# Layer 0's values from the copied projection, and one transposition for the source terms of four blocks

## The chip, the cores and the metric

The kernel runs on one core of a Trainium2 chip. The metric is device time in microseconds (us), from one launch to its end; several runs are taken and the median counts.

## What is computed

Two layers of attention on a graph, over a batch of 16 images with 1024 nodes of 256 features each. `adj` is a 1024 x 1024 matrix of zeros and ones per image.

```python
# layer 0: x = layernorm(x + gnn0(x, adj))
h = einsum('bnd,hde->bhne', x, W)                    # 4 heads of 64
e_src = einsum('bhne,hte->bhtn', h, a_src)           # source terms
e_dst = einsum('bhne,hte->bhtn', h, a_dst)
weight = where(adj == 1, leaky_relu(e_src[..., :, None] + e_dst[..., None, :], 0.01), -1e9)
dst = softmax(weight) @ h + bias
out = relu(dst) + h                                  # then a layer norm per head
# layer 1: x = layernorm(x + gnn1(x, adj))
qkv = layer_norm(x).split_heads(8)                   # queries, keys and values are the same
attn = softmax(where(adj > 0, qkv @ qkv.T / sqrt(32), -inf)) @ qkv
x = x + attn
x = x + gelu(layer_norm(x) @ W1 + b1) @ W2 + b2
```

The kernel uses that exp(leaky_relu(s + d)) is a maximum of two products: after a factor common to a row is taken out, a weight of layer 0 is max(cb, dinv) * mask, where cb comes from the source terms (`exp(0.99 * e_src)`, a row over the queries, the same on all partitions) and dinv from the destination terms (`exp(-0.99 * e_dst)`, one number per partition). The values of layer 0 are `(h + bias) * exp(e_dst)` for each head, with `exp(e_dst)` itself as a 65th column that gives the sums.

## The kernel before

**Streams.** The program is written out in Python for all 16 images. Two generators, `layer0` and `layer1`, are interleaved by a loop at the end of `fast_path` (lines 1014 to 1032): while layer 1 of image b runs (`attention1`, then `mlp`), layer 0 of image b + 1 runs beside it (`prepare`, then `attention0`). The loop asks a model of the engines, the class `Pace` (lines 90 to 173), which of the two can go on, and follows a course (`COURSE`, line 999) that says how far layer 0 should be for each place of layer 1. Shorter pieces, called chains, are begun with `begin` and run when `Pace` believes that what they need is there (`advance`), or at once when somebody needs their result or their buffer (`complete`, `settle`). The order on each engine is then fixed: the engines work off their queues in that order and wait on semaphores. All engines' instructions are recorded on line 61, so the profile names tiles and not lines.

**Layer 0, prepare** (lines 484 to 540) goes over the eight blocks of 128 nodes of an image in pairs (`GB` = 2):
- four transposes of x to `xT` on TensorE, copied by ScalarE;
- `turn_mask` for each block: eight transposes of the adjacency block `ak`, and a ScalarE instruction that writes the mask; it also issues the load of a later adjacency block on GpSimd's queue;
- for each block, two matmuls of `xT` with `w0e` give a bank `ph` of 264 columns: h (256), the destination terms (4), the source terms (4). ScalarE takes from it, in this order, the source terms, `exp` of the destination terms twice, and h into `hb`;
- `values0` on VectorE: an add (tile `z`) and a multiplication into `v0`;
- `turn_sources` after each pair: makes rows out of the source terms, takes their exponential and stores them to `esr` in DRAM on SyncE's queue. After four blocks the first two factors `cb` are loaded back from `esr`, spread over all partitions (`spread_factor`).

The banks of PSUM that prepare uses are two, `acc0` and `acc1` (`bank0`, lines 370 to 375); `attention0`'s accumulation, the transposes of layer 1's outputs (tiles `oT`, `o`) and of its normalised inputs (`sq`) use the same two. Tiles that carry chains are completed before their bank is taken again. The framework orders any two engines' accesses to one bank.

**Layer 0, attention0** (lines 567 to 626): VectorE makes 128 x 512 weights `p` from cb, dinv and mask, and TensorE multiplies them with `v0` into `acc`. `residual0` and `after0` do the head norms and the norm ahead of layer 1.

**Layer 1, attention1** (lines 722 to 804): 32 steps an image, each of four logits matmuls into `ps`, four exponentials on ScalarE, two mask products on VectorE and the products into `po`, three steps behind. Then `mlp`, with `hid`.

In the trace each image has a turn, where `mlp` of one image ends and `attention1` of the next begins, and prepare starts at about the same place.

Of the kernel before, what the change touches and what calls it, by code (L numbers as in the profile page):

```python
# [31 lines left out]
F32 = mybir.dt.float32  # L32
# [3 lines left out]
AF = mybir.ActivationFunctionType  # L36
# [3 lines left out]
P = 128  # L40
# [136 lines left out]
def fast_path(  # L177
# [24 lines left out]
    nc = Pace(tc.nc)  # L202
    B, N, D = x.shape
    H0, _, HO = w0.shape
# [9 lines left out]
    BPH = HALF // P  # L214
    Q = 32
# [3 lines left out]
    GB = 2  # L219
# [6 lines left out]
    const = ctx.enter_context(tc.tile_pool(name="const", bufs=1))  # L226
    def ring(name, bufs, **kwargs):
        return Ring(nc, ctx.enter_context(tc.tile_pool(name=name, bufs=bufs, **kwargs)), bufs)

    one, two, three, four, eight = [  # L230
        ring(n, i) for n, i in (("one", 1), ("two", 2), ("three", 3), ("four", 4), ("eight", 8))
    ]
# [11 lines left out]
    ident = const.tile([P, P], F32, name="ident")  # L244
# [22 lines left out]
    for c in range(DC):  # L267
        for h in range(H0):
            nc.scalar.dma_start(w0e[:, c, h * HO : (h + 1) * HO], w0[h, c * P : (c + 1) * P, :])

    apart = [const.tile([P, H0, Q], F32, name=f"apart{g}") for g in range(GB)]
    for t in apart:
        nc.vector.memset(t, 0.0)
    terms = ((a_src, nc.sync, w0e[:, :, D + H0 : D + 2 * H0]), (a_dst, nc.scalar, w0e[:, :, D : D + H0]))

    at = one.tile([P, 3, PAIR, HO, T], F32, name="v0")
    vectors = [at[:, i, :, :, :] for i in range(3)] + [one.tile([P, PAIR, HO, T], F32, name="xl")]
    for i, (src, queue, _) in enumerate(terms):
        for pair in range(H0 // PAIR):
# [3 lines left out]
                    tensor=src.tensor,  # L283
# [5 lines left out]
    def rows(queue, src, name):  # L289
        t = const.tile([P, D], F32, name=name)  # L290
        queue.dma_start(t, bass.AP(tensor=src.tensor, offset=src.offset, ap=[[0, P], [1, D]]))
        return t

    bias0_r = rows(nc.scalar, bias0, "bias0_r")
    for i, (_, _, dst) in enumerate(terms):
        for c in range(DC):
            t = two.tile([P, H0, HO], F32, name="z")
# [72 lines left out]
    def bank0(shape, dtype=F32):  # L370
        i = min((i for i in range(2) if not banks0[i]["busy"]), key=lambda i: banks0[i]["taken"])
        for chain in banks0[i]["readers"]:
            complete(chain)
        banks0[i].update(readers=[], taken=1 + max(bank["taken"] for bank in banks0))
        return ps_a.tile(shape, dtype, f"acc{i}"), banks0[i]
# [13 lines left out]
    def transpose_rows(dst, src, scale=None, shift=None):  # L389

        pt = side_bank([P, DC, GB, P])
        for g in range(GB):
            for c in range(DC):
                nc.tensor.transpose(pt[:, c, g, :], src[:, g, c * P : (c + 1) * P], ident)
        pt = pt.rearrange("p c g q -> p c (g q)")
        if scale is None:
            nc.scalar.copy(dst, pt)
        else:
            for c in range(DC):
                nc.scalar.activation(  # L400
                    dst[:, c, :], pt[:, c, :], AF.Identity, bias=shift[:, c : c + 1], scale=scale[:, c : c + 1]
                )
# [13 lines left out]
    def uses(chain, tile):  # L416
        users.setdefault(tile, []).append(chain)
# [13 lines left out]
    def begin(chain, engine, *needs):  # L431
        for n in needs:
            if not callable(n):
                uses(chain, n.tensor.name)
        chains.append([chain, engine, needs])

    def run(item):
        running.append(item[0])
        step = next(item[0], None)
        running.pop()  # L440
        if step is None:
            chains.remove(item)
        else:
            item[1:] = step[0], step[1:]
# [13 lines left out]
    def complete(chain):  # L458

        for item in list(chains):  # L460
            if item[0] is chain:
                while item in chains:
                    run(item)
# [8 lines left out]
    def load_adj(i):  # L472
        b, k = divmod(i, NB)
        if b < B:
            ak = adj_blocks[i] = three.tile([P, N], BF16, name="ak")
            nc.gpsimd.dma_start(ak, adj[b, k * P : (k + 1) * P, :])

    def load_blocks(i):
        b, k = divmod(i, NB // GB)
        if b < B:  # L480
            xk = x_blocks[i] = two.tile([P, GB, D], F32, name="xk")
            load_x(xk, b, k * GB, GB)

    def prepare(b, hb, esr, cbs, v0, dinv, mask):

        def turn_mask(k):
            i = b * NB + k  # L490
            ak = adj_blocks.pop(i)
            pt, _ = bank0([P, NB, P], BF16)
            for j in range(NB):
                nc.tensor.transpose(pt[:, j, :], ak[:, j * P : (j + 1) * P], identb)
            nc.scalar.activation(
                mask[k // BPH][:, :, k % BPH * P : (k % BPH + 1) * P],
                pt,
                AF.Square,
                bias=shift_c,
                scale=-(NEAR0 + NEAR1),  # L500
                accum_out=types[:, i : i + 1],
            )
            load_adj(i + 3)

        turning, scaling = [], []
        for k in range(0, NB, GB):
            i = b * (NB // GB) + k // GB
            load_blocks(i + 1)
            xk = x_blocks.pop(i)
            xT = one.tile([P, DC, GB * P], F32, name="xT")  # L510
            transpose_rows(xT, xk)
            yield 0.45, bank0_ready
            turn_mask(k)
            yield 0.5, bank0_ready, xT
            if k % BPH == 0:

                finish_norms(b - 1, k // BPH)
                hb.append(one.tile([P, BPH, D], F32, name=f"hb{k // BPH}"))
            for g in range(GB):
                if g == 0:  # L520

                    for chain in turning:
                        complete(chain)
                ph, _ = bank0([P, D + 2 * H0])
                for c in range(DC):
                    nc.tensor.matmul(ph, xT[:, c, g * P : (g + 1) * P], w0e[:, c, :], start=c == 0, stop=c == DC - 1)
                nc.scalar.copy(apart[g][:, :, 0], ph[:, D + H0 : D + 2 * H0])
                nc.scalar.activation(v0[:, k + g, :, HO], ph[:, D : D + H0], AF.Exp)
                nc.scalar.activation(dinv[:, k + g, :], ph[:, D : D + H0], AF.Exp, scale=-0.99)
                scaling.append(values0(v0[:, k + g, :, :], ph))  # L530
                begin(scaling[-1], "vector", ph)
                nc.scalar.copy(hb[-1][:, (k + g) % BPH, :], ph[:, 0:D])
                yield 0.9, bank0_ready
                if g == 0:
                    turn_mask(k + 1)
                    yield 0.5, bank0_ready, xT
            turning.append(turn_sources(esr, k, cbs))
            begin(turning[-1], "tensor", bank0_ready, *apart)
        for chain in turning + scaling:
            complete(chain)  # L540

    def turn_sources(esr, k, cbs):
        es, _ = bank0([P, GB, P])
        for g in range(GB):
            nc.tensor.transpose(es[:, g, :], apart[g].rearrange("p h q -> p (h q)"), ident)
        rows = two.tile([P, GB * P], F32, name="rows")
        nc.scalar.activation(rows, es.rearrange("p g q -> p (g q)"), AF.Exp, scale=0.99)
        nc.sync.dma_start(esr[:, k * P : (k + GB) * P], rows[0:P:Q, :])
        if k + GB == BPH:
            for at in ((0, 0), (0, 1)):  # L550
                cbs[at] = spread_factor(esr, *at)
        yield from ()

    def values0(v, ph):
        t = two.tile([P, H0, HO], F32, name="z")
        nc.vector.tensor_add(t.rearrange("p h e -> p (h e)"), ph[:, 0:D], bias0_r)
        nc.vector.tensor_mul(v[:, :, 0:HO], t, v[:, :, HO : HO + 1].to_broadcast([P, H0, HO]))
        yield from ()

    def spread_factor(esr, n, pair):  # L560

        cb = two.tile([P, PAIR, HALF], F32, name="cb")
        rows = esr[pair * PAIR : (pair + 1) * PAIR, n * HALF : (n + 1) * HALF]
        nc.sync.dma_start(cb, bass.AP(tensor=rows.tensor, offset=rows.offset, ap=[[0, P], [N, PAIR], [1, HALF]]))
        return cb
# [374 lines left out]
    def finish_norms(b, n):  # L940
        for chain in [c for at, c in norms.items() if at[:2] == (b, n)]:
            complete(chain)
# [537 lines left out]
```

## Time and profile before

| what | us |
|---|---|
| median of 3 runs | 3459.49 |
| lowest and highest of the runs | 3459.29, 3473.02 |
| the profiled execution | 3472.71 |
| its span, first to last instruction | 3470.9 |
| mean granted clock of TensorE | 0.979 of full speed |
| TensorE busy | 3321.2 |
| VectorE busy | 2982.8 |
| ScalarE busy | 1937.3 |

How to read the profile: PE is TensorE's matmul, PEld its loading of weights, DVE VectorE, ACT ScalarE, POOL GpSimd, SP SyncE. A group of instructions is written as output tile, arrow, input tiles, with shape and count, then busy time in us and the mean of one in ns, then the idle time of its engine just before, with what ended it. "The waits" are sums of that idle time by who waited and who ended it, with the number of times and the longest. "The chain" is followed back from the last instruction: at each step to what released it. A busy TensorE is not TensorE at its peak, since a matmul that waits in the pipeline counts as busy. Times within an execution count from the span's start.

### The profile page before, as it was taken

The numbers are of one execution on the slowest core, as the hardware profiler recorded it, in microseconds if no ns is written. First come the engines' busy times: TensorE is split into PE (matmuls) and PEld (weight loads), VectorE is DVE, ScalarE is ACT, GpSimd is POOL, SyncE is SP. The second block draws the span as 40 slices with busy tenths as digits, with TensorE's granted clock in tenths as the row PEclk, the third lists the DMA queues.
The fourth block names the chain that finished last, engine by engine and source line by source line (L and its number), as shares of the span: only waits on it lengthen the run. The fifth ranks groups of instructions, "written<-read, shape, count | busy, mean of one in ns | idle before, by whom it ended". The sixth has DMA issues, their size and how long they took to land.

```text
span 3470.9 us, 141029 instructions
## 1 busy us (share of the span) xinstructions
PE 3321.2 (96%) x64161; PEld 2259.7 (65%) x64161; DVE 2982.8 (86%) x5262; ACT 1937.3 (56%) x4192; POOL 418.9 (12%) x424
## 2 busy tenths in 40 slices
PE   5799999999999999999999999999999999999998
PEld 5458576675856758576585766757667585765846
DVE  5898898988979898898988989889898888989873
ACT  2563846547375573745638466473655737466363
POOL 1102011010110101101020110101101011010200
PEclk9899999999999999999999999999999999999999
DMA  5211202011020111202112020120201112020000
GB/s 135 50 22 37 47 25 58 15 44 40 28 59 21 41 34 33 56 18 58 23 35 48 24 57 18 41 43 27 60 20 40 37 31 59 20 54 10 26 3 14
DMA packets 95727, 131.30 MB, mean 38 GB/s; under 512 B 10384, under 2 KB 61584, under 8 KB 95120
## 3 DMA queue, kind: packets, MB, share of 16 engines
q1 hardware_dynamic: 75104, 87.58, 8.2%
q0 software_dynamic: 18432, 33.56, 6.7%
q8 instruction: 504, 8.26, 1.0%
q10 hardware_dynamic: 1584, 1.05, 0.1%
q14 instruction: 103, 0.84, 0.1%
HBM read 138.68 MB, written 17.04 MB: 45 GB/s over the span
## 4 chain that ended last, share of the span: by engine, by line
PE 72%; DVE 20%; ACT 5%; issue 2%; DMA 0%; POOL 0%; ACTq 0%; POOLq 0%; DVEq 0%
PE po L61 28%; PE ps L61 25%; PE acc L61 19%; DVE p L61 15%; ACT p L61 2%; DVE o L61 1%; DVE x L61 1%; ACT sq L61 1%; DVE st L61 1%; DVE z L61 1%; ACT mask L61 1%; ACT hb L61 1%; DMA w0e<-in_L_gnn_W_dram 0%; DVE v L61 0%; ACT z L61 0%
## 5 line engine op out<-in xcount | busy, mean ns | idle before, releaser
L61 ACT ACTIVATE p<-ps 128x512 f32<-128x512 f32 x2048 | 1061.9, 615 | 403.5 <-PE ps L61 374.8
L61 DVE TENSOR_TENSOR p<-p,mask 128x1024 f32<-128x1024 f32 x1024 | 1187.4, 1219 | 11.9 <-ACT p L61 11.9
L61 DVE SCALAR_TENSOR_TENSOR p<-cb,dinv,mask 128x512 f32<-128x512 f32 x1024 | 711.7, 746 | 0.1
L61 PE MATMUL ps<-nT 32*128 32x512 f32 x4096 | 687.1, 655 | 2.2 <-ACT p L61 2.2
L61 ACT ACTIVATE hid<-ps,b_sb 128x256 f32<-128x256 f32 x512 | 242.6, 474 | 794.9 <-PE ps L61 793.7
L61 PEld LDWEIGHTS po<-v,p 128*32 128x32 f32 x32768 | 395.5, 110 | 335.3 <-issue 287.1
L61 PE MATMUL acc<-v,p 128*64 128x65 f32 x16384 | 563.1, 227 | 33.6 <-DVE p L61 15.8
L61 PEld LDWEIGHTS acc<-v,p 128*64 128x64 f32 x16384 | 517.0, 140 | 114.4 <-issue 55.6
L61 PE MATMUL po<-p,v 128*32 128x512 f32 x2048 | 553.6, 616 | 0.0
L61 PE MATMUL po<-p,unit 128*32 128x512 f32 x2048 | 553.1, 615 | 0.0
L61 PE MATMUL ps<-yT,w_sb 128*128 128x256 f32 x2048 | 489.8, 385 | 0.0
L61 PE MATMUL po<-w_sb,hid 128*128 128x256 f32 x2048 | 474.6, 384 | 0.0
L61 PEld LDWEIGHTS po<-w_sb,hid 128*128 128x128 f32 x2048 | 382.1, 190 | 54.0
L61 PEld LDWEIGHTS ps<-yT,w_sb 128*128 128x128 f32 x2048 | 376.0, 190 | 51.1
L61 PE MATMUL po<-v,p 128*32 128x33 f32 x32768 | 391.1, 198 | 13.5 <-issue 9.6
L61 PEld LDWEIGHTS ps<-nT 32*128 32x128 f32 x4096 | 227.3, 187 | 104.9 <-issue 41.7
L61 PEld LDWEIGHTS po<-p,v 128*32 128x32 f32 x2048 | 78.6, 109 | 332.1 <-issue 174.6
L61 POOL TENSOR_TENSOR r<-v,mhalf 128x1 f32<-128x1 f32 (+1 forms) x192 | 157.9, 831 | 706.4 <-DVE v L61 624.5
L61 DVE TENSOR_TENSOR z<-acc,bias_r 128x256 f32<-128x256 f32 x128 | 54.2, 424 | 183.5 <-ACT hb L61 183.3
L61 PE MATMUL acc<-w0e,xT 128*128 128x264 f32 x512 | 152.1, 421 | 38.4 <-DVE z L61 23.0
L61 POOL DMA_DIRECT2D ak<-in_adj_dram x128 | 69.7, 545 | 974.6 <-PE acc L61 962.0
L61 POOL TENSOR_TENSOR r<-v1s,mhalf 128x4 f32<-128x4 f32 x32 | 61.5, 1923 | 992.0 <-DVE v1s L61 992.0
(108 smaller groups left out, 2745.6 us busy)
## 6 DMA issues: line engine op xcount, KB each, us to landing
ak<-in_adj_dram POOLq DMA_DIRECT2D x128, 256.0 KB, 3.9
cb<-esr SPq DMA_DIRECT2D x64, 512.0 KB
xk<-in_x_dram SPq DMA_DIRECT2D x64, 256.0 KB
xl<-in_x_dram SPq DMA_DIRECT2D x32, 512.0 KB
out_dram<-z SPq DMA_DIRECT2D x128, 128.0 KB
w_sb<-in_L_gnn_W_dram SPq DMA_DIRECT2D x2, 1024.0 KB
esr<-rows SPq DMA_DIRECT2D x64, 4.0 KB
v<-in_L_gnn_a_src_dram SPq DMA_DIRECT2D x2, 320.0 KB
```

The costliest lines, as they stand in the source:

```text
L61: return method(*args, **kwargs)
```

## The change

There are two edits in `prepare` and its helpers.

1. `values0` no longer reads h from the bank `ph` but from ScalarE's copy in `hb`. ScalarE's copy is now written ahead of the chain in the program, and the chain is begun on `hb`.
2. The source terms of four blocks are gathered in a tile `es` of 128 x 4 x 4 and turned by one transposition of 128 x 16 to 16 x 128, once per half of the queries, instead of four transposes of 128 x 128 (two per pair of blocks) in which the four terms stood 32 columns apart (`apart`). The exponential goes over 16 x 128 in place of 128 x 256 for each pair, and the rows are stored by four DMAs of 4 x 128 per half in place of two of 4 x 256. The tiles `apart`, their two memsets, and the completion of the chain ahead of a pair's first matmul are gone.

Since the order is worked out by `Pace`, the streams are interleaved a little differently with these edits.

```diff
-    apart = [const.tile([P, H0, Q], F32, name=f"apart{g}") for g in range(GB)]
-    for t in apart:
-        nc.vector.memset(t, 0.0)
...
             for g in range(GB):
-                if g == 0:
-
-                    for chain in turning:
-                        complete(chain)
                 ph, _ = bank0([P, D + 2 * H0])
                 for c in range(DC):
                     nc.tensor.matmul(ph, xT[:, c, g * P : (g + 1) * P], w0e[:, c, :], start=c == 0, stop=c == DC - 1)
-                nc.scalar.copy(apart[g][:, :, 0], ph[:, D + H0 : D + 2 * H0])
+                if (k + g) % BPH == 0:
+                    es = two.tile([P, BPH, H0], F32, name="es")
+                nc.scalar.copy(es[:, (k + g) % BPH, :], ph[:, D + H0 : D + 2 * H0])
                 nc.scalar.activation(v0[:, k + g, :, HO], ph[:, D : D + H0], AF.Exp)
                 nc.scalar.activation(dinv[:, k + g, :], ph[:, D : D + H0], AF.Exp, scale=-0.99)
-                scaling.append(values0(v0[:, k + g, :, :], ph))
-                begin(scaling[-1], "vector", ph)
-                nc.scalar.copy(hb[-1][:, (k + g) % BPH, :], ph[:, 0:D])
+                h = hb[-1][:, (k + g) % BPH, :]
+                nc.scalar.copy(h, ph[:, 0:D])
+                scaling.append(values0(v0[:, k + g, :, :], h))
+                begin(scaling[-1], "vector", h)
                 yield 0.9, bank0_ready
...
-            turning.append(turn_sources(esr, k, cbs))
-            begin(turning[-1], "tensor", bank0_ready, *apart)
+            if (k + GB) % BPH == 0:
+                turning.append(turn_sources(es, esr, k // BPH, cbs))
+                begin(turning[-1], "tensor", bank0_ready, es)
...
-    def turn_sources(esr, k, cbs):
-        es, _ = bank0([P, GB, P])
-        for g in range(GB):
-            nc.tensor.transpose(es[:, g, :], apart[g].rearrange("p h q -> p (h q)"), ident)
-        rows = two.tile([P, GB * P], F32, name="rows")
-        nc.scalar.activation(rows, es.rearrange("p g q -> p (g q)"), AF.Exp, scale=0.99)
-        nc.sync.dma_start(esr[:, k * P : (k + GB) * P], rows[0:P:Q, :])
-        if k + GB == BPH:
+    def turn_sources(es, esr, n, cbs):
+        pt, _ = bank0([BPH * H0, P])
+        nc.tensor.transpose(pt, es.rearrange("p g h -> p (g h)"), ident)
+        rows = two.tile([BPH * H0, P], F32, name="rows")
+        nc.scalar.activation(rows, pt, AF.Exp, scale=0.99)
+        for g in range(BPH):
+            at = (n * BPH + g) * P
+            nc.sync.dma_start(esr[:, at : at + P], rows[g * H0 : (g + 1) * H0, :])
+        if n == 0:
             for at in ((0, 0), (0, 1)):
                 cbs[at] = spread_factor(esr, *at)
...
-    def values0(v, ph):
+    def values0(v, h):
         t = two.tile([P, H0, HO], F32, name="z")
-        nc.vector.tensor_add(t.rearrange("p h e -> p (h e)"), ph[:, 0:D], bias0_r)
+        nc.vector.tensor_add(t.rearrange("p h e -> p (h e)"), h, bias0_r)
         nc.vector.tensor_mul(v[:, :, 0:HO], t, v[:, :, HO : HO + 1].to_broadcast([P, H0, HO]))
```

## The prediction

> **What bounds the kernel now.** I read the page's busy times and chain first, then the waits, then the groups that the edits touch, then one image turn (970 to 1054 us) on the engines' timelines.
>
> ```profile
> PE 3321.2 (96%) x64161; PEld 2259.7 (65%) x64161; DVE 2982.8 (86%) x5262; ACT 1937.3 (56%) x4192; POOL 418.9 (12%) x424
> ...
> PE 72%; DVE 20%; ACT 5%; issue 2%; DMA 0%; POOL 0%; ACTq 0%; POOLq 0%; DVEq 0%
> ```
>
> TensorE carries the chain, so work taken off it counts where it is dense. Next, who waits for whom (us in total, times, longest):
>
> ```profile
> DVE z L61 <- ACT hb L61: 183.3, 92, 3.3
> ...
> PEld acc L61 <- DVE z L61: 54.2, 33, 2.2
> ...
> PE acc L61 <- DVE z L61: 42.5, 37, 2.3
> ```
>
> `z` is the add of values0. It waits for ScalarE's copy of h although both only read the bank, and TensorE then waits for `z` to have the bank: 42.5 us. The groups that go or shrink:
>
> ```profile
> L61 PE MATMUL acc<-ident,apart 128*128 128x128 f32 x128 | 27.8, 301 | 0.2 <-ACT apart L61 0.2
> ...
> L61 ACT ACTIVATE rows<-acc 128x256 f32<-128x256 f32 x64 | 26.2, 410 | 0.0
> ```
>
> The chain where an image's attention1 begins (start, us, what): ScalarE carries it for 9 us, then `z`, then TensorE.
>
> ```profile
> 977.32 1.95 ACT sq L61 x4
> ...
> 979.94 0.27 ACT hb L61
> 980.21 0.02 issue
> 980.24 0.44 DVE z L61
> 980.67 0.04 issue
> 980.72 0.65 PE acc L61 x4
> 981.37 2.92 PE ps L61 x7
> ```
>
> TensorE idles there twice (1.40 and 1.64 us, both for `z`), and its clock answers. In these windows the number after the engines is the granted clock:
>
> ```profile
> 978.00:980.00 2.00, 1.07 (x9) 0.42 (x4) 0.57 (x1) 2.00 (x9) 0.00 (x0) 1.00 0.31 55
> 980.00:982.00 2.00, 1.28 (x9) 0.99 (x10) 1.73 (x3) 2.00 (x6) 0.00 (x0) 0.97 0.18 66
> 982.00:984.00 2.00, 2.00 (x6) 0.61 (x3) 2.00 (x6) 2.00 (x6) 0.00 (x0) 0.50 0.00 0
> 984.00:988.00 4.00, 4.00 (x78) 2.41 (x78) 3.93 (x9) 1.94 (x4) 0.00 (x0) 0.50 0.02 4
> 988.00:989.00 1.00, 1.00 (x7) 0.52 (x9) 1.00 (x4) 0.83 (x2) 0.00 (x0) 0.65 0.00 0
> ```
>
> Half clock from 981.9 to 988.7, 6.8 us. Windows over the whole span show such stretches at every one of the 15 turns. From copy to copy of `ranges<-v` (once an image) the period is 211.0 to 211.8 us at seven turns, where the half-clock stretch is 6.8 us, and 208.0 to 208.7 at four, where it is 3.4. These are 62 and 61 times 3.413.
>
> [...] `z` from the bank takes 424 ns, `v<-z,v` with all operands in SBUF 425. I take no change for `z`. [...] Here the load of cb starts 2.06 us after the issue of the esr store ends (37.94 to 40.00).
>
> **Values from the copy.** The wait of `z` for the copy stays, now for the data, in the same place in VectorE's queue at most turns: of the 183 us I credit nothing. What goes is TensorE's wait for `z`: the bank is free 0.46 us earlier (add 0.42, hand-over 0.04). In the steady turns the first of the two idles (1.40 us) lies under ScalarE, which is busy from 971.3 to 985.9 without a gap, so it is worth nothing; the second is on the chain.
>
> **The turn, re-ordered.** The instruction order of the changed kernel shows more: prepare now runs one step ahead. The transposes of the next x block and its mask block stand before the two `sq` transposes, and one products step moves behind them. On ScalarE, after the copy at 980.21, come xT 0.48, four exponentials 1.95, mask 1.11, two nT 0.90, exponentials 1.95, two nT 0.90 = 7.29, so the fifth group of exponentials can start at 987.5, against 989.71 now: 2.2 us earlier, with a mask (1.11 on ScalarE, 0.55 on TensorE) done that came later. Against it: TensorE has one gap of about 2.8 us (third logits end near 977.4, the mask transposes wait for the copy at 980.2) in place of two of half that, so the half clock won't vanish. Both ends: 2.6 gained, or 1.0 lost if a whole window of half clock (1.7 us of work) falls later, into dense products, less 0.7. I take 1.5 gained. Queued behind the mask transposes in that gap are an `sq` transposition and the fourth logits, and ScalarE's nT waits for the former; both are in the list above. The step that moves also issues a load of x on SyncE, now ahead of one output store instead of behind it (0.33 us, nobody waits for the store), and one of the adjacency on GpSimd, whose queue waits 962 us in all for acc: no cost.
>
> **Source terms by one transpose.** Per image, eight 128x128 transposes go. Their price in a dense stretch: four xk and two apart take 0.81 us from start to the next group (1005.12 to 1005.93), four oT 0.59, so two cost 0.22 and eight 0.88. Two transposes of 128x16 come. No row shows one: below, 0.11 as its 128 columns stream alike; above, 0.25 with the change of shape that the lone pair shows (0.36 at 1050.52, 0.14 over 0.22). I take 0.18: 0.88 - 0.36 = 0.52 gained, ends 0.38 and 0.66. ScalarE loses 64 evictions of 373 to 390 ns and gains 32 of half the width, 0.2 to 0.3 each: some 17 us of busy time, under TensorE except in the prologue. The two memsets were done by 2.2 us, far ahead of 23: nothing.
>
> **Stores.** Per half, two stores of 0.48 to 0.61 us become four, so SyncE issues 64 more, 32 us in all, and cb is asked for some 1.0 us later. Behind them stand xk (needed a block, 20 us, later) and cb (issued at 1008.6, first used at 1053.7): covered by 45 us. Without that cover it would cost those 1.0 to 1.5 us once an image.
>
> **The first image.** Nothing overlaps prepare between 23 and 48.8 us. Per pair of blocks TensorE waits twice 0.73 for `z` and 1.07 for the mask, because apart holds the other bank. Of this 2 x 0.46 goes four times and 1.07 three times: 6.9. But the cb load is asked for 1.5 us later relative to its block, DMA is full there (share over 1.0 at 42 to 48), and ScalarE fills up next. I take 4, between 1 and 7.
>
> **The sum.** The profiled execution took 3472.7 us (span 3470.9), 13.2 above the median 3459.5 and within the three runs' 3459.3 to 3473.0; 13.2 is four steps of 3.4, so runs seem to differ in how many turns are the long kind. Gain: 15 x (1.5 + 0.52) + 4 = 34. From the profile's execution 3438, from the median 3425. If the period instead settles at 208.2 at all 14 intervals (they sum to 2947.2 now, 2914.8 then) the profile's execution gives 3472.7 - 4 - 32.4 = 3436. I predict 3431; own range 3419 to 3441.
>
> **Rivals.**
> - Only the removed work counts, the turn gives nothing: 3459.5 - 4 - 15 x 0.52 = 3448. For: ScalarE carries the turn. Against: its list is 2.2 us shorter up to the fifth group.
> - The other side: the 2.8 us gap makes every turn the long kind, 62 steps. Fifteen turns of 6.8 us half clock swallow the saved work, as the period steps by 3.4: 14 x 211.6 = 2962.4, so 3472.7 + 15.2 - 4 = 3484. [...] For: eight of 15 do now. Against: mask and x transposes add work around the gap.
> - The change does nothing at the bound (the waits move to `hb`, transposes hide): 3459.
> - Even 60 steps: 14 x 204.8 = 2867 gives 3472.7 - 4 - 80 = 3389. It needs the upper end at each turn and a vanished half clock.
>
> **Chances.** Forecast 0.52, removed work only 0.22, slower rival 0.12, nothing 0.06, 60 steps 0.08. The range 3406 to 3465 takes in the first, second and fourth (0.80): its low end is 3459.5 - 7 - 15 x (2.6 + 0.5) = 3406, its high end "nothing" plus half of the spread between runs. A measurement of this kernel tells about 0.5%, 17 us, from no change: faster than 3442 is 0.50 of the forecast and the 0.08; slower than 3477 is 0.10 of its rival; the rest 0.32.
>
> **What would show it.** The wait of acc for `z` gone from TensorE, one for `hb` of a few us in its place; 32 transposes `es` under 0.3 us; the first cb product near 45 us; periods of 208 or less, and a mean clock above 0.979. Periods of 211.6 throughout, or TensorE waiting for `hb` over 3 us a turn, would make it wrong.

## The result and the profile after

| | before | after |
|---|---|---|
| median of 20 runs each, us | 3464.02 | 3458.47 |
| lowest to highest | 3452.80 to 3473.62 | 3452.70 to 3465.96 |
| ratio, 95% interval | | 0.9983 (0.9972 to 0.9994) |
| the profiled execution, us | 3472.71 | 3452.70 |
| span, mean granted clock | 3470.9, 0.979 | 3450.8, 0.979 |

The change won 5.6 us in the median, 0.17%: inside the wide range of the prediction (3406 to 3465), but outside its own range (3419 to 3441) and a sixth of the 34 us of its sum. The two profiled executions lie 20.0 us apart, because that of before ran 8.7 above its median and that of after 5.8 below (it was the fastest of its 20); so single executions are compared below by stages, and sums of them are not taken for the result.

The page after, busy times and shares of the chain. The work of the transposes and evictions is gone (96 matmuls, 17 us of ScalarE), yet TensorE is busy 5 us more:

```profile
PE 3326.3 (96%) x64065; PEld 2264.1 (66%) x64065; DVE 2978.1 (86%) x5260; ACT 1920.6 (56%) x4160; POOL 418.8 (12%) x424
...
PE 72%; DVE 20%; ACT 4%; issue 2%; DMA 1%; POOL 0%; SPq 0%; POOLq 0%; DVEq 0%; ACTq 0%
```

The waits after (us in total, times, longest). The first stays, as forecast; the second stands where 42.5 us for `z` stood:

```profile
DVE z L61 <- ACT hb L61: 183.0, 82, 3.7
...
PE acc L61 <- ACT hb L61: 25.7, 17, 1.8
```

The new groups, by shape:

```profile
L61 PE MATMUL acc<-ident,es 128*16 128x128 f32 x32 | 8.8, 274 | 0.3 <-ACT es L61 0.3
L61 ACT ACTIVATE rows<-acc 16x128 f32<-16x128 f32 x32 | 8.2, 256 | 0.0
```

The chain at one image's turn, which begins at 1168.06. ScalarE carries it to `hb` as before, and `z` is gone from it; behind it come the transposes of the next mask, logits that take 3.32 us, and first products that take 2.60:

```profile
1175.27 1.94 ACT sq L61 x4
...
1177.89 0.27 ACT hb L61
1178.16 0.04 issue
1178.20 1.19 PE acc L61 x12
1179.40 3.32 PE ps L61 x7
1182.72 1.04 PE acc L61 x4
1183.76 2.60 PE po L61 x70
```

The windows of the same turn, 0 to 6, 6 to 10, 10 to 14, 14 to 18 and 18 to 22 us from its first logits. Behind the five engines stands the granted clock. It is half from about 11 to 18 us, as it was before (981.9 to 988.7 is 12 to 19 us from that turn's first logits, at 970.10):

```profile
1168.06:1174.06 6.00, 6.00 (x38) 3.61 (x38) 5.41 (x25) 4.84 (x13) 3.61 (x5) 1.00 0.29 87
1174.06:1178.06 4.00, 2.38 (x8) 1.12 (x9) 4.00 (x5) 4.00 (x13) 0.00 (x0) 1.00 0.75 164
1178.06:1182.06 4.00, 3.85 (x20) 2.67 (x19) 3.91 (x7) 4.00 (x10) 0.53 (x1) 0.64 0.43 87
1182.06:1186.06 4.00, 4.00 (x66) 1.77 (x68) 3.96 (x10) 3.40 (x8) 0.00 (x0) 0.51 0.09 16
1186.06:1190.06 4.00, 4.00 (x122) 2.15 (x112) 1.49 (x4) 2.06 (x4) 0.00 (x0) 1.00 0.02 4
```

**Where the time is.** I cut each image from ScalarE's load of the exponential table, with which its attention1 starts, to VectorE's copy `ranges<-v`, and from there on to the next such load. The second part stayed (122.3 us before, 122.2 after, means of 14). The first, "the stage" from here on, went from 88.17 to 87.55 us. Its lowest value, at turns whose half clock lasts 3.4 us, rose from 86.29 to 86.46: the changed kernel's best turns are slower. In the first image, from the first w0e matmul to the first weights, 25.8 us became 23.0.

From the first weights to the first turn, 285.6 us became 278.9. Most of this lies in the first image's attention1, which no `mlp` precedes: from its first logits to `ranges<-v` it took 88.8 us before and 83.5 after. The runs below repeat it: 84.0 in e1 and 83.9 in e7, which have the new order and `z` from the copy, 86.6 in e6, 86.7 in e3, 88.1 to 89.7 in the other kernels of the old order, and 100.8 in e4 with its idle matmuls. Why this one place gains was not looked into.

### The profile page after: what moved, and what is told of

Read it like the earlier page. It is cut to its first block, busy times and chain, and to the rows that moved or that the text cites. A ratio compares the mean times of both kernels' runs of the same rounds, so it can differ in the third digit from the quotient of the medians.

```text
span 3450.8 us, 140756 instructions
## 1 busy us (share of the span) xinstructions
PE 3326.3 (96%) x64065; PEld 2264.1 (66%) x64065; DVE 2978.1 (86%) x5260; ACT 1920.6 (56%) x4160; POOL 418.8 (12%) x424
## 4 chain that ended last, share of the span: by engine, by line
PE 72%; DVE 20%; ACT 4%; issue 2%; DMA 1%; POOL 0%; SPq 0%; POOLq 0%; DVEq 0%; ACTq 0%
PE po L61 28%; PE ps L61 25%; PE acc L61 19%; DVE p L61 16%; ACT p L61 2%; DVE o L61 1%; ACT sq L61 1%; DVE st L61 1%; DVE x L61 1%; ACT mask L61 0%; ACT z L61 0%; DVE v L61 0%; DVE hb L61 0%; DVE z L61 0%; DVE mv L61 0%
## 5 line engine op out<-in xcount | busy, mean ns | idle before, releaser
L61 DVE TENSOR_TENSOR p<-p,mask 128x1024 f32<-128x1024 f32 x1024 | 1187.0, 1217 | 12.2 <-ACT p L61 11.1
L61 PE MATMUL ps<-nT 32*128 32x512 f32 x4096 | 707.3, 654 | 2.6 <-ACT p L61 2.3
L61 PEld LDWEIGHTS ps<-nT 32*128 32x128 f32 x4096 | 243.9, 187 | 108.2 <-ACT p L61 41.7
L61 DVE TENSOR_TENSOR z<-hb,bias_r 128x256 f32<-128x256 f32 x128 | 54.0, 422 | 183.0 <-ACT hb L61 183.0
L61 POOL TENSOR_TENSOR r<-v0s,mhalf 128x8 f32<-128x8 f32 x64 | 129.2, 2019 | 367.0 <-DVE v0s L61 367.0
```

Source lines behind the costliest of these rows:

```text
L61: return method(*args, **kwargs)
```

## The experiments

All were timed in five rounds, beside runs of the kernel before on the same chip. "Order" is that of the instructions at the turn: old as before, or new as in the changed kernel. "z from" is what `values0` reads on the chip. "Idle" are matmuls of constants whose outputs are overwritten. The stage is the mean of 14 images of the profiled execution, with the lowest; "half" is the number of those turns with 6.8 us or more of half clock, of 14. Runs e1 to e4, e5 to e8, e9 to e11 and e12 were made on four chips, so across these groups only ratios are compared. The profiled execution was its kernel's slowest in e4 and e6, and its fastest in e7, e8 and e10.

| kernel | order | z from | source terms | idle | ratio (95%) | stage (lowest) | half |
|---|---|---|---|---|---|---|---|
| before | old | bank | eight transposes | | 1 | 88.17 (86.29) | 9 |
| after | new | copy | two | | 0.9983 (0.9972 to 0.9994) | 87.55 (86.46) | 9 |
| e1_values | new | copy | eight | | 1.0019 (1.0009 to 1.0028) | 89.03 (87.81) | 14 |
| e2_rows | old | bank | two | | 0.9944 (0.9924 to 0.9964) | 86.47 (85.87) | 3 |
| e3_held | old | copy | two | | 1.0008 (0.9997 to 1.0018) | 88.15 (87.22) | 12 |
| e5_copy_old | old | copy | two | | 1.0020 (1.0008 to 1.0032) | 88.14 (87.31) | 12 |
| e6_bank_new | new | bank | two | | 0.9952 (0.9937 to 0.9966) | 87.30 (86.48) | 5 |
| e12_idle_back | old | copy, idle put back | two | 64 of one column | 1.0006 (0.9992 to 1.0021) | 88.20 (86.33) | 12 |
| e8_rows_pad | old | bank | two + eight idle | | 1.0054 (1.0038 to 1.0069) | 87.90 (86.42) | 7 |
| e4_warm | new | copy | two | 11, 6 of them between logits | 1.0496 (1.0472 to 1.0520) | 99.13 (96.22) | all |
| e7_fill | new | copy | two | 7 | 0.9952 (0.9937 to 0.9966) | 86.73 (86.46) | 0 |
| e9_fill_copy_old | old | copy | two | 5 | 0.9938 (0.9921 to 0.9955) | 86.07 (85.88) | 0 |
| e10_fill_rows | old | bank | two | 5 | 0.9950 (0.9932 to 0.9967) | 86.13 (85.87) | 0 |
| e11_fill_before | old | bank | eight | 5 | 0.9977 (0.9967 to 0.9988) | 86.71 (86.27) | 0 |

**The edits alone.** My first theory was that the re-ordering only moves work and is worth nothing; its rivals, the prediction's own pricing, the half clock, and a re-ordering that loses.

```diff
# e1_values: from before
-                scaling.append(values0(v0[:, k + g, :, :], ph))
-                begin(scaling[-1], "vector", ph)
-                nc.scalar.copy(hb[-1][:, (k + g) % BPH, :], ph[:, 0:D])
+                h = hb[-1][:, (k + g) % BPH, :]
+                nc.scalar.copy(h, ph[:, 0:D])
+                scaling.append(values0(v0[:, k + g, :, :], h))
+                begin(scaling[-1], "vector", h)
# e2_rows: from after, the same lines the other way round
# e3_held: from after, for the planner only
-                begin(scaling[-1], "vector", h)
+                begin(scaling[-1], "vector", ph)
...
+        nc.read[ph.tensor.name] = max(nc.read.get(ph.tensor.name, 0.0), nc.free["vector"])
```

> Values from ScalarE's copy alone; the source terms stay as before (apart, two transposes a pair of blocks). Its order at the turn is that of the changed kernel (x and mask transposes of the next blocks ahead of the sq transposes), with the apart transposes between the second sq block and the first products. The prediction's pricing (re-order 1.5 us a turn, a share of the first image): 3464 - 22 - 2, about 3440, ratio 0.993. Theory 1, the re-ordering only moves work from the dense part into the ramp and is worth nothing: attention1 from its first exponentials to the next factors copy stays at 88.2 us in the mean, only the first image gains 1 to 3 us, ratio 0.999 to 1.000. Theory 3, the re-ordering is a loss that the transposes pay for: ratio 1.001 to 1.003.

> One transpose for half of the queries alone; values still from the bank. The order at the turn is the old one without the apart transposes; the mask of block 2 follows its x transposes directly. Prediction's pricing of this part (0.52 us an image, a share of the first image): 3464 - 8 - 2, about 3454, ratio 0.997. Theory 1 (transposes partly beside other work): 0.997 to 0.999. Theory 3 (transposes worth their full price, re-ordering a loss): 0.996 to 0.998, as fast as the changed kernel or faster. If the transposes are wholly hidden: 0.999 to 1.000 with no change of the stages' means.

> The changed kernel, with the planner told that the bank is held until the values are made. On the chip z still reads the copy; only the instruction order differs: at the turn it is the old order, the same as in the kernel with the rows edit alone. Theory 1 (re-ordering worth nothing): the time of the changed kernel within 0.1 per cent, ratio 0.997 to 0.999. The prediction's pricing (re-ordering gains 1.5 a turn): 22 us slower than the changed kernel, ratio 1.005. Theory 3 (re-ordering a loss): 3 to 8 us faster than the changed kernel, 0.996.

The values edit alone cost 6.6 us, the rows edit alone won 21.3, more than any theory had said and nearly four times the whole change. With the old order and z from the copy the gain was gone again. Two kernels of one order at the turn, e2 and e3, lay 23 us apart: so it was not the order alone, and my first theory fell.

**One wait.** The planner's orders of e2 and e3 still differed in the first image and in one place an image away from the turn. So e5 keeps e2's order exactly, and e6 the changed kernel's (one small swap in the first image apart); only the operand that `z` reads differs.

```diff
# e5_copy_old, from e2_rows (the planner still books the read of ph)
-        nc.vector.tensor_add(t.rearrange("p h e -> p (h e)"), ph[:, 0:D], bias0_r)
+        nc.enter("vector", "tensor_add", (t2, ph[:, 0:D], bias0_r), {})
+        nc.nc.vector.tensor_add(t2, h, bias0_r)
# e6_bank_new, from after
-        nc.vector.tensor_add(t.rearrange("p h e -> p (h e)"), h, bias0_r)
+        nc.enter("vector", "tensor_add", (t2, h, bias0_r), {})
+        nc.nc.vector.tensor_add(t2, ph[:, 0:D], bias0_r)
```

> The kernel with the rows edit alone (3443 us, 0.9944), every engine's instruction order kept exactly, only z reads ScalarE's copy in place of the bank. So one thing differs on the chip: TensorE no longer waits for z (1.40 us at the second product with w0e of a turn, 0.39 at the sq transposes). The prediction's pricing (wait gone, worth 0 to 0.46 a turn): 3436 to 3443, ratio 0.992 to 0.9945. New theory, the thin stretch of TensorE moves later: without the wait the second w0e product runs 1.46 us earlier, the thin stretch comes later, behind the third logits, and the half clock that follows it falls on the first products instead of on work that waits for ScalarE: half clock from about 11 to 18 us after the turn's first logits in most turns, instead of 6 to 10 us; first products done 1 to 1.5 us later; ratio 0.999 to 1.001.

> The changed kernel, its instruction order kept (one small swap in the first image apart), only z reads the bank again. New theory (the wait for z spaces TensorE's work so that the half clock comes early and costs little): part of it comes back, half clock starting 2 to 4 us sooner in the turns than in the changed kernel, ratio 0.993 to 0.997. If instead the order is what costs, and the source of z nothing: as the changed kernel, 0.997 to 0.999. The prediction's pricing (the wait at the bank costs 0.46 a turn): 7 us slower than the changed kernel, 1.000.

Taking TensorE's wait for `z` away cost 0.76% in the old order (e2 to e5, 0.9944 to 1.0020) and 0.31% in the new one (e6 to after). A wait was worth keeping. TensorE at one turn of e2 (start, us, group, and in brackets the idle time before it):

```profile
1384.14 1.79 PE L61 MATMUL ps<-nT 32*128 32x512 f32 x8
1387.34 1.28 PE L61 MATMUL acc<-w0e,xT 128*128 128x264 f32 x4 [1.41 <-DVE z L61]
1388.55 2.31 PE L61 MATMUL ps<-nT 32*128 32x512 f32 x8
...
1394.69 0.62 PE L61 MATMUL po<-p,v 128*32 128x512 f32 x1
```

And at one of e5, where the second w0e matmuls come 1.47 us sooner in the turn (4.33 against 5.80 us from its start, at 1595.03 and 1381.54) and the first products 0.97 later (14.12 against 13.15), each at 1.06 us instead of 0.62:

```profile
1597.64 1.79 PE L61 MATMUL ps<-nT 32*128 32x512 f32 x8
1599.36 1.16 PE L61 MATMUL acc<-w0e,xT 128*128 128x264 f32 x4
1600.84 2.58 PE L61 MATMUL ps<-nT 32*128 32x512 f32 x8 [0.32 <-ACT p L61]
...
1609.15 1.06 PE L61 MATMUL po<-p,v 128*32 128x512 f32 x1
```

The windows say why, e2 first, at 6, 10 and 14 us from the turn's start. In e2 the half clock falls on the stretch where TensorE waits for ScalarE anyway; the products run at full clock:

```profile
1387.54:1391.54 4.00, 4.00 (x16) 1.93 (x15) 2.47 (x3) 4.00 (x13) 0.00 (x0) 0.59 0.60 102
1391.54:1395.54 4.00, 3.71 (x22) 1.59 (x24) 3.85 (x8) 4.00 (x10) 0.00 (x0) 0.99 0.10 33
1395.54:1399.54 4.00, 4.00 (x121) 2.45 (x115) 3.93 (x9) 4.00 (x10) 0.53 (x1) 1.00 0.37 79
```

In e5 that stretch is at full clock, and the half clock falls on the products:

```profile
1601.03:1605.03 4.00, 2.98 (x12) 1.40 (x11) 2.47 (x3) 4.00 (x13) 0.00 (x0) 1.00 0.58 98
1605.03:1609.03 4.00, 3.84 (x12) 2.29 (x12) 3.83 (x8) 4.00 (x10) 0.00 (x0) 0.60 0.10 33
1609.03:1613.03 4.00, 4.00 (x83) 2.49 (x83) 3.93 (x8) 1.88 (x5) 0.00 (x0) 0.55 0.01 4
```

So it is at most turns: in e2 the half clock starts 5.7 to 6.7 us into the turn and lasts 3.4 us in 11 of 14; in e5 it never starts before 8.5 and lasts 6.8 in 12 of 14. The idle for `z` seems to make TensorE's thin stretch begin early; the last experiment below asks whether it does.

In e6 the ratio is as the new theory had it, but the turns are so only in part. The half clock starts before 7.1 us at 4 of 14 turns (in the changed kernel never before 9.0). At the other ten it starts at 10.4 to 12.3 us, as late as in the changed kernel, but at six of them it lasts 3.4 us. Why it is shorter there stays open.

**The clock itself.** If the removed wait costs through the half clock only, it must cost nothing at full clock. The first try to keep the clock up put idle matmuls between the logits:

```diff
# e4_warm, from after: in exponentials, at the third and fourth group of a turn
                 nc.tensor.matmul(tiles[e], of_keys[q, quad, keys], of_queries[q, quad, :], start=True, stop=True)
+                if spare:
+                    fill(spare[0], 96)
# and fill(spare[0], 256, 256, 256) behind the third group
```

> The changed kernel with idle matmuls of constants at the turn (128x128 weights, 8 x 96 and 3 x 256 columns, 2.6 us at full clock, into the bank that the first products overwrite), put where TensorE waits for ScalarE: behind each logits matmul of the third and fourth group, and three behind the third group. Nothing of the result depends on them. Theory 2, the half clock is what eats the re-ordering's gain: stretches of half clock at the turn shrink from 3.4 or 6.8 us to 0 or 3.4, the first products take 1.3 instead of 2.6 us, the fifth exponentials start 1 to 2 us earlier and each turn gains 1.5 to 3: 3458 - 25 to 45, ratio 0.985 to 0.992. Theory 1, ScalarE's list sets the turn whatever the clock is: the ratio stays at 0.997 to 0.999. If the idle matmuls delay the logits or the clock doesn't answer to them: 1.000 to 1.005.

It missed by far: 5% slower, where the last of its theories, idle matmuls that delay the logits, had allowed 0.5%. TensorE's first rows of that third group show that it is this one. Each of these matmuls stands as two records (x2), and the idle ones have a line of their own:

```profile
1237.09 1.12 PE L61 MATMUL ps<-nT 32*128 32x512 f32 x2
1238.14 0.46 PE L754 MATMUL po<-w0e,ident 128*128 128x96 f32 x2
1238.53 1.12 PE L61 MATMUL ps<-nT 32*128 32x512 f32 x2
1239.58 0.46 PE L754 MATMUL po<-w0e,ident 128*128 128x96 f32 x2
```

One logits matmul of 32 rows takes 1.12 us, and four in a row take 1.14 (1231.23 in the same turn): they run side by side, and a 128-row matmul between them ends that. A logits matmul with its idle one takes 1.44 us from start to start, so eight take 11.5 where two groups took 2.3. These 9.2 us more, an estimate at full clock, are of the size of the 9.8 by which the lowest stage grew. So e7 fills around the groups only, with 128 x 128 by 256 columns:

```diff
# e7_fill, from after: at attention1's steps
             if i == 2:
+                spare.append(ps_o.tile([P, HALF], F32, name="po"))
+                fill(2)
+            if i == 3:
+                fill(2)
...
                 ready[i] = exponentials(*steps[i])
+                if i == 2:
+                    fill(3)
```

> The changed kernel with idle matmuls of constants (128x128 weights, 256 columns, 0.43 us each at full clock) where TensorE would wait for ScalarE: two ahead of the third logits, three behind them, two ahead of the fourth; none between logits of one group, which run side by side. Their outputs are overwritten. Half clock as the thing that costs: stretches of half clock behind 9 us into the turn shrink or vanish (lost clock time of a turn under 1.7 us, against 1.7 to 3.4), the first products take 1.3 us and end 1 to 2 us sooner; ratio 0.985 to 0.993. If ScalarE's list alone sets the turn: 0.997 to 0.999 although the clock is full. If the idle matmuls hold up the logits: over 1.000.

No half clock was left at any of the 14 turns, and the changed kernel went from 0.9983 to 0.9952. The timed runs agree: the mean granted clock was 0.991 to 0.993 in all six, and 0.976 to 0.984 in the runs of before beside them. Three more put the idle matmuls (2, 2 and 1) into the old order:

> Old order, one transpose a half, z from the copy (1.0020 without fill), with idle matmuls of 128x128 by 256 columns at the turn: two ahead of the third logits, two behind them, one ahead of the fourth. If the removed wait for z costs only through the half clock: at full clock it costs nothing and may win; from first exponentials to the next factors copy 85.3 to 85.9 us at every image, ratio 0.990 to 0.993, as the rows edit or faster. If the wait's removal costs by something else (ScalarE or VectorE collide): 86.5 to 88, ratio 0.996 to 1.002. The prediction's 0.46 for the wait on the path would show as 85.4 against the rows edit's 85.88 in its short kind.

> The rows edit alone (z from the bank, 0.9944) with the same idle matmuls. The idle of 1.40 us for z at the second product with w0e isn't filled, so an early half clock may stay, at 6 to 10 us. 85.7 to 86.1 us at nearly every image instead of 85.88 at eleven of fourteen; ratio 0.991 to 0.994. If the idle matmuls then run at half clock and hold up the third logits: 0.995 to 0.998.

> The kernel before with the same idle matmuls. With the long kind of turn gone, every image takes the short kind's 86.3 us: periods 208.0 to 208.8 instead of 210.5 in the mean, ratio 0.991 to 0.995. Its distance from the rows edit with the same idle matmuls prices the transposes alone, at one clock: 0.41 us an image (6 us, 0.002) by the two short kinds, 0.52 by the prediction. If the kinds of turn have nothing to do with it: 0.999 to 1.001.

In e9 no half clock was left either. In e10 three turns and in e11 four keep 3.4 us of it, from 5.7 to 6.7 us on, behind the wait for `z` that nothing fills there; at them the stage is 86.5 to 86.6 in e10. All four ratios are above what had been expected of them. For e11 part of the reason is that its forecast was worked out from the profiled execution of before, 8.7 us above the median; the rest was not looked into.

At full clock z's source makes no difference: the first `po<-v,p` matmuls stand 14.05 us into the turn with the copy (e9), 14.03 with the bank (e10), and the stage is 85.88 in both at undisturbed turns. The ratios of the two don't part either, so the 0.76% between e2 and e5 was the half clock's. e9 is the fastest of all in the median (3433.47 us beside 3458.10 of before and 3436.45 of e10), though its interval doesn't part it from e10. Its windows at 10 and 14 us:

```profile
1385.37:1389.37 4.00, 3.85 (x22) 1.86 (x26) 3.84 (x8) 4.00 (x10) 0.00 (x0) 1.00 0.10 33
1389.37:1393.37 4.00, 4.00 (x120) 2.44 (x113) 3.93 (x8) 4.00 (x9) 0.53 (x1) 1.00 0.39 80
```

**A little more work.** Does the rows edit win by what it removes?

```diff
# e8_rows_pad, from e2_rows: in transpose_rows as prepare calls it
+        for g in range(pad):
+            nc.nc.tensor.transpose(pt[:, 0, g, :], src[:, g, 0:P], ident)
```

> The kernel with the rows edit alone, with two idle 128x128 transposes put ahead of each block pair's x transposes (eight an image, about 0.88 us of TensorE, overwritten by the real ones; none of the eviction, the stores or the waits of before). If the transposes' TensorE time is what the rows edit won (0.52 an image, 8 us in all): slower than the rows edit by 8 to 13 us, ratio 0.997 to 0.998. If the period locks to 61 windows of the clock, so that work below one window is free as long as the lock holds: as the rows edit, 0.994 to 0.996, periods still near 208.2. If 0.9 us is enough to fall out of the lock: the long kind at most turns, periods 210.5 to 211.8, ratio 0.999 to 1.001.

It cost 1.1%, some 38 us by the ratios, more than any expectation. At turns of 3.4 us half clock the stage rose by 0.55 us (85.87 to 86.42), which is 8 us in all. Most of the rest shows as more turns with 6.8 us (7 for 3), at which the stage is 89.0 to 89.8: with these, 1.43 us in the mean, 20 over the 14 images, of the 24.8 us between the two profiled executions. The timed runs of e8 have a median 8 us above its profiled one, and what their turns look like wasn't seen.

**The idle put back.** If the early idle alone brings the early half clock, another wait in the same place must do.

```diff
# e12_idle_back, from e5_copy_old: ahead of the second block's products with w0e
# (made holds the z tiles in order, ph is the bank that the product overwrites)
+                if g == 1:
+                    nc.nc.tensor.matmul(ph[:, 0:1], ident, made[-1][:, 0:1], start=True, stop=True)
```

> The kernel with the old order and z from the copy (1.0020), with TensorE's idle at the second product with w0e of each pair of blocks put back by another way: a matmul of one column that reads the z of the block before, into the bank that the product then overwrites. Nothing waits at the bank for z; the data wait gives the same idle of about 1.4 us at the turn, and 64 small matmuls are added. If the idle's place is what puts the half clock early, as read from the wait at the bank: half clock from 5.5 to 6.5 us on for 3.4 us in most turns, second w0e product at 5.8 us again, ratio 0.994 to 0.997 although there is more work. If the wait at the bank does something else (the later wait of the sq transposes for z, which isn't put back): as without it, 1.000 to 1.004.

The idle is there (start, us, group, idle before). The ratio misses the forecast and lies where the other theory had it, that the wait at the bank does something else, perhaps through the later wait of the `sq` transposes, which isn't put back:

```profile
1393.71 0.35 PE L518 MATMUL acc<-z,ident 128*128 128x1 f32 x2 [1.49 <-DVE z L559]
1393.92 1.14 PE L61 MATMUL acc<-w0e,xT 128*128 128x264 f32 x4
```

But the turns are of two sorts now. In 6 of 14 the half clock starts 5.6 to 7.2 us into the turn, which none of e5's did, and the stage is 86.3 to 86.9; in the other 8 it starts at 11.6 to 12.2 and the stage is 89.1 to 90.3, worse than e5's 87.3 to 89.9. So the idle makes the early half clock possible and does not keep it. What keeps it in e2 is open: the later wait of the `sq` transposes wasn't tried.

Drift against the clock's own steps is another reading. In the clock records of the traces of before and after each stretch of half clock (26 and 23 of them) begins a whole number of steps of 3.4133 us after the first one, to within 0.003 us; from the first to the last of before it is 3413.33 us, 1000 steps. e2's early turns follow each other at 208.25 us in the mean (965.66 to 2006.91, five images), which is 61 times 3.413 and little more; e8's, with 0.55 us more in the stage, at 208.57 (1392.99 to 2018.71, three images). e8's turns fall out of the early kind after one to four, e12's after one to three, e2's after seven. Against it: the last four turns of before are early ones, with 0.43 us more in the stage than e2's, and follow each other at 208.21 (2453.89 to 3078.52). So a longer stage need not make a longer period, and the drift was not varied by itself.

## Why the prediction was wrong

**The failed step is "The turn, re-ordered": 1.5 us gained a turn, 22 of the 34 us.** At one clock the re-ordering loses some 0.6 us: the stage is 86.46 in e7 against 85.88 in e9. e7 has two idle matmuls more, but the distance is much the same without any: 86.48 to 86.64 at three turns of e6 against 85.87 to 85.92 at eleven of e2, both with `z` from the bank, where the half clock comes early and lasts 3.4 us. The first products come 1.1 us later into the turn, 14.27 in e7 against 13.16 in e9. First logits and first products of one turn each, e7 above:

```profile
1374.27 1.14 PE L61 MATMUL ps<-nT 32*128 32x512 f32 x8
1388.54 0.62 PE L61 MATMUL po<-p,v 128*32 128x512 f32 x1
...
1375.37 1.14 PE L61 MATMUL ps<-nT 32*128 32x512 f32 x8
1388.53 0.62 PE L61 MATMUL po<-p,v 128*32 128x512 f32 x1
```

Two things were wrong in the step.

First, the yardstick. I set ScalarE's list, which let the fifth group of exponentials start at 987.5, against 989.71 in the trace, and called 2.2 us the order's. But 989.71 was a turn with 6.8 us of half clock, and ScalarE was idle before it, 0.67 us, for TensorE. The same trace had turns of the other kind. ScalarE at the turn that starts at 2662.00:

```profile
2675.59 2.25 ACT L61 ACTIVATE p<-ps 128x512 f32<-128x512 f32 x4
2677.50 0.81 ACT L61 COPY xT<-acc 128x512 f32<-128x512 f32 x1
2677.97 0.63 ACT L61 ACTIVATE rows<-acc 128x256 f32<-128x256 f32 x1
2678.69 2.06 ACT L61 ACTIVATE p<-ps 128x512 f32<-128x512 f32 x4
```

There the fifth group starts 16.69 us into the turn without any idle, in the old order. With one transposition a half and full clock it starts at 17.05 in the old order (e10) and at 17.05 in the new one (e7): the order moves it by nothing. At the turn of after shown above it starts at 19.39:

```profile
1184.21 1.25 ACT L61 ACTIVATE nT<-acc,be_c,g_c 128x256 f32<-128x256 f32 x2
1187.45 2.06 ACT L61 ACTIVATE p<-ps 128x512 f32<-128x512 f32 x4 [1.99 <-PE ps L61]
```

ScalarE finished its list in time, at 1185.46 or 17.40 us into the turn, as I had worked out, and then waited 1.99 us for a TensorE at half clock.

Second, the trade. Up to the first products ScalarE bounds the turn; behind them TensorE does: at the turn of before from 2662.00, whose first products start at 2675.17, ScalarE has no idle over 0.1 us from 2663.16 to 2680.75 while TensorE idles 1.41 and 0.36 us for `z`, and from 2676 to 2692 TensorE is busy for 4.00 of each 4 us. The new order puts xT and mask (1.59 us of ScalarE by the prediction's rows) ahead of that point and takes their transposes (1.03 us of TensorE at a turn of e2, from the first transposition of x at 1188.24 to the next logits at 1189.27) out of the stretch behind it: 0.56 us lost, an estimate from these two sums. Measured are 1.1 us lost up to the first products and 0.5 won back behind them. So the estimate has the kind right and both sizes too high, and that its difference fits is in part luck. The step looked only at the gain.

**Values from the copy** was credited nothing for z's wait, which is right (183.3 to 183.0 us). TensorE's wait, 0.46 us, was put "on the chain". At full clock it is worth nothing (14.05 and 14.03). Without idle matmuls it is a loss of 0.76%, some 26 us, in the old order. The prediction had the place of this ("if a whole window of half clock falls later, into dense products"), as the low end of a step that it then took at +1.5; and its slower rival asked for the long kind at every turn, which e1 shows (14 of 14; 0.19% slower). In the changed kernel 9 of 14 turns are of it, as before.

**Source terms by one transpose**: 0.52 us an image, measured 0.40 at one clock (86.27 in e11, 85.87 in e10). The two transposes take 0.27 us each by their rows, 0.36 was allowed for both; the step was right in kind and a quarter too high. Eight idle 128 x 128 transposes cost 0.55 in e8, where eight had been priced at 0.88. The rows edit alone nevertheless won 21 us, with the early half clock at most of its turns.

**Stores**: four take about 1.3 us a half (0.26 to 0.34 each; 0.48 to 0.61 had been allowed), hidden but in the first image, where VectorE waits 1.53 us for cb after the change and 2.37 in e2. **The first image**: 4 us forecast, 2.8 found up to the first weights. The 6.8 us behind them, up to the first turn, had no term.

**The terms together**, per image in the stage of the profiled executions: transposes -0.40, re-ordering +0.58, half clock -0.80 (before 88.17 less its 86.28 at full clock is 1.89; after 87.55 less 86.46 is 1.09): -0.62, the difference of the means by construction. The last term is that of two executions and not the change's. At one clock the two edits together lose 0.18 us an image, 2.5 over 14. From the first w0e matmul to the first turn 311.4 us became 301.9, and with idle matmuls 311.2 (e11) and 303.3 (e7). So the 5.6 us were, as an estimate from these sums, won ahead of the first turn and not at the turns, for which the prediction had 30 of its 34.

Of its signs, the wait for `hb` (1.8 us at the longest), the transposes (274 ns) and the first weights (43.9 us) came. The mean clock stayed at 0.979, and the periods ran from 208.0 to 211.7.

**The periods** were read rightly: turns of before with 6.8 us follow each other at 211.61 us in the mean (970.10 to 2028.17, five images), 62 times 3.413. But I used them to round a gain, where a turn's cost depends on where the half clock falls in it: the lowest stage is 85.87 us with it at 6 to 10 us into the turn (e2) and 87.31 with it never before 8.5 (e5). Nor is a period near 61 steps a sign that the clock holds it there: in e9, without any half clock, it is 208.26 in the mean (335.11 to 3250.70). The idles that go with the half clock are short: none of TensorE's is over 1.8 us at the turns shown, and with idle matmuls in its waits e7 and e9 had no half clock left at any of the 14 turns.

## What to carry to other kernels

A wait on the critical engine can be worth keeping where that engine's clock answers to its idles, as here: without TensorE's wait for `z` the half clock fell on the products and cost 0.76% (e2 to e5), and idle matmuls took the half clock away (e7, e9). Before you take a wait away, ask which stretch becomes the thin one and what runs in the next. When you measure a list of instructions against the trace, take the yardstick from a turn at full clock, and look for turns of both kinds in the one trace. Then price at one clock: idle matmuls that keep it up, placed where TensorE waits anyway, gave clean steps of 0.4 and 0.6 us where the timed ratios mixed the edits with the clock, and with the old order and both edits they gave the fastest median here.

## What the runs showed of the hardware

- Half clock without a long idle: at the turns shown no idle of TensorE is over 1.8 us, yet the clock falls for 3.4 or 6.8 us; five idle matmuls in e9, some 2.4 us (two take 0.96 there, from 1380.68 to 1381.64), were enough to prevent it. With `z` from the bank the same five left 3.4 us of it at 3 of 14 turns (e10) and at 4 (e11).
- A half clock can be free: the stage is 85.87 us with 3.4 us of it at 6 to 10 us into the turn (e2), and 85.88 without any (e9). At three turns of e10, with idle matmuls to do, the same stretch costs 0.6 to 0.7 us.
- Four matmuls with 32 rows and 512 columns take 1.14 us together and 1.12 each when a 128-row matmul separates them (e4).
- A transpose of 128 x 16 takes 273 ns in the median, no less than one of 128 x 128 (273); its weights take 88 ns against 140.
